# Last image's second layer: corners summed by TensorE, table writes reordered, experts' products issued ahead

## The chip, the cores and the metric

The kernel runs on one core of a Trainium2 chip. The metric is device time in microseconds (us). A core has five engines with queues of their own: TensorE (PE; its weight loads are listed apart as PEld), VectorE (DVE), ScalarE (ACT), GpSimd (POOL) and SyncE (SP), which here issues most transfers. Sixteen DMA engines move the data of all queues. TensorE reads SBUF and writes PSUM; VectorE and ScalarE read both. All data are fp32; a product of fp32 matrices shows as two matmul instructions, called passes here, and a transpose as one.

## The reference, cut to what matters

The program is two layers over 8 images of 128 channels and 32 x 32 positions (1024 tokens). The first layer (attention and a spectral mixer) takes most of the time and isn't touched. The second layer, for one image, is:

```python
# deformable convolution: 3 taps a token, 4 corners a tap, bilinear weights times a mask
h = layer_norm(x)                                  # over channels
offset, mask = conv1x3(h, off_w), sigmoid(conv1x3(h, mask_w))
for tap in range(3):
    samp = sum(corner_weight[k] * h[corner_row[k]] for k in range(4)) * mask[tap]
    out += samp @ conv_w[tap]
x = x + out + conv_b
# mixture of 8 experts, two of them kept for each token
t = layer_norm(x)
p = softmax(t @ router_w + router_b);  keep the two largest, scaled to sum 1
x = x + sum(p[e] * (t @ expert_w[e] + expert_b[e]) for e in the two)
```

## The kernel before, in words

The weights of the convolution are applied before sampling: for each tap, all tokens' `h @ conv_w[tap]` is written to a table in DRAM (`tab[tap]`, one for each tap), in four copies shifted by 0, 1, 32 and 33 rows, so that one row of 2 KB holds the four corners of a sampling point. Sampling one tap for a tile of 128 tokens is then one indirect DMA (a gather) of 128 rows of 2 KB, and a weighted sum of its four corners.

Tokens are worked on in NT = 8 tiles of 128. Second layers of images 0 to 6 run as generators between the spectral stage's instructions. The last image has no cover: when the spectral stage is over, `image` runs alone. Instructions are issued in the order of the program text; each engine takes its own in that order, and semaphores order what touches the same tile. Its steps, with the lines that matter:

- `points` turns `x2` back to tokens (`tok`), normalises, and computes `gs` (a product and a ScalarE copy, L1040, for each tile). After the fourth and the eighth tile twelve table writes each are put on a list, `write` (L1030) issues them on SP, four at a time, sorted by tap within the list as it stands. So they go out as first half tap 0, 1, 2, then second half tap 0, 1, 2. `corners` computes row numbers `idx` and weights `w`.
- `sampled` with `alone` calls `by_taps`. Its order is the first tap of all eight tiles, then taps 1 and 2 of tile 0, of tile 1 and so on: 24 points. `fetch` issues a gather (L1192, POOL) into one of three `g` tiles of three slots, some five ahead. Two points in three are added by VectorE, four `scalar_tensor_tensor` each (L1217); every third has its corners scaled by ScalarE (L1200), then a reduction (L1213) and an add (L1214).
- `norm_steps` takes statistics of the sums (L788, L789) and the inverse root on VectorE (L770 to L778), and normalises (L795). `turn_steps` transposes (L920) and copies (L923).
- `gates` makes the router's logits (L1240), the softmax and the two largest on VectorE, and turns the gates (L1275, L1277).
- Experts: for each tile two products of 512 columns into two PSUM banks `p_e` (L1137). ScalarE scales four experts of one bank (L1144), VectorE the four of the other (L1149), then reduces eight to one (L1154) and adds (L1157). After four tiles the expert biases (L1166) and the turned sums (L1169) are added up in a bank `p_out`, copied (L1173) and stored, 256 KB at a time (L1174).

The spectral stage's own accumulator is `po`, one PSUM tile of two banks (pool `op`, one buffer); its halves are copied out by ScalarE (L1585) and VectorE (L1586).

Of the kernel before, what the change touches and what calls it, by code (L numbers as in the profile page):

```python
# [11 lines left out]
F32 = mybir.dt.float32  # L12
# [6 lines left out]
P = 128  # L19
B = 8  # L20
# [782 lines left out]
class DeformAndExperts:  # L803
# [179 lines left out]
        got.extend((idx, w))  # L983
        yield

    def image(self, b, x2, x1):

        got = []
        yield from self.points(b, x2, got, True, x1)
        yield from self.sampled(b, got, True)  # L990

    def residual(self, b):

# [10 lines left out]
    def points(self, b, x2, got, alone, x1):  # L1004


        nc, sb = self.nc, self.sb
        newton = nc.vector if alone else nc.gpsimd
        tok = sb.tile([P, NT, C], F32, tag="tok", name="tok")
        yield from self.turn_back(x2, tok, x1)  # L1010
        yield
        ht = sb.tile([P, NT, C], F32, tag="ht", name="ht")
        yield from norm_steps(nc, sb, tok, ht, 1e-6, newton, not alone)
        yield 1.0 if alone else 5.0
        hc = sb.tile([C, T], F32, tag="hc", name="hc")
        yield from self.turn_steps(ht, hc)
        nc.gpsimd.tensor_tensor(tok, tok, self.cb.unsqueeze(1).to_broadcast([P, NT, C]), ALU.add)
        yield


        tab = self.tabs[b % 2]
        N = TAPS * C + TAPS * 9
        gs = sb.tile([P, NT, N], F32, tag="gs", name="gs", bufs=1)
        writes = []

        def write():
            if writes:
                i0, tap, slot, back = writes.pop(0)
                r0 = 33 - back + i0 * P
                nc.sync.dma_start(  # L1030
                    tab[tap][r0 : r0 + 4 * P, slot, :].rearrange("(i p) c -> p i c", p=P),
                    gs[:, i0 : i0 + 4, tap * C : (tap + 1) * C],
                )

        for i in range(NT):
            pg = self.bank("p_g")
            nc.tensor.matmul(
                pg[:, 0:N], hc[:, i * P : (i + 1) * P], self.gw, start=True, stop=True
            )
            nc.scalar.copy(gs[:, i, :], pg[:, 0:N])  # L1040
            if i % 4 == 3:
                writes += [
                    (i - 3, tap, slot, back)
                    for tap in range(TAPS) for slot, back in enumerate((0, 1, 32, 33))
                ]
                if alone:
                    writes.sort(key=lambda w: w[1])
            for _ in range(4 if alone else 2):
                write()
            yield 1.0 if alone else 1.5  # L1050
        while writes:
            for _ in range(4 if alone else 2):
                write()
            yield 1.0 if alone else 1.7
        po = self.bank("p_om")
        for tap in range(TAPS):
            at = TAPS * C + 9 * tap
            nc.tensor.matmul(
                po[:, 0 : 9 * NT], self.shift[tap], gs[:, :, at : at + 9],
                start=(tap == 0), stop=(tap == TAPS - 1),  # L1060
            )
        om = sb.tile([P, NT, 9], F32, tag="om", name="om")
        nc.vector.tensor_tensor(
            om, po[:, 0 : 9 * NT].rearrange("p (i k) -> p i k", k=9), self.base, ALU.add
        )
        yield
        yield from self.corners(om, got)
        got.append(tok)

    def sampled(self, b, got, alone):  # L1070

        nc, sb = self.nc, self.sb
        newton = nc.vector if alone else nc.gpsimd
        idx, w, tok = got
        x3 = sb.tile([P, NT, C], F32, tag="x3", name="x3")
        rows = [tab.rearrange("r s c -> r (s c)") for tab in self.tabs[b % 2]]
        if alone:
            yield from self.by_taps(idx, w, tok, x3, rows)  # L1080
        points = [] if alone else [(i, tap) for i in range(NT) for tap in range(TAPS)]
        fetched, here, tiles = [], [], []

        def fetch():
# [10 lines left out]
                )  # L1095
                fetched.append((i, tap))

        if not alone:
            yield 8.0
            for _ in range(4):  # L1100
                fetch()
                yield 2.6
            yield 5.0
        for i, tap in points:
            fetch()
            g = tiles[i]
# [13 lines left out]
                nc.vector.tensor_add(x3[:, i, :], x3[:, i, :], tok[:, i, :])  # L1120
            yield 2.6
        tt = sb.tile([P, NT, C], F32, tag="ht", name="tt")
        yield from norm_steps(nc, sb, x3, tt, 1e-5, newton, not alone)
        yield 1.0 if alone else 5.0
        tc = sb.tile([C, T], F32, tag="hc", name="tc")
        yield from self.turn_steps(tt, tc)
        yield
        got = []
        yield from self.gates(tc, got, 0.0 if alone else 3.0)
        gate, gt = got  # L1130
        ot = sb.tile([C, T], F32, tag="ht", name="ot")
        for i in range(NT):
            g = sb.tile([P, TAPS, 4, C], F32, tag="g", name="ge", bufs=3)
            part = g.rearrange("p t k c -> p (t k) c")[:, 0:NE]
            for grp in range(2):
                pe = self.bank("p_e")
                nc.tensor.matmul(  # L1137
                    pe, tc[:, i * P : (i + 1) * P],
                    self.ew[:, grp * 4 : grp * 4 + 4, :].rearrange("d e c -> d (e c)"),
                    start=True, stop=True,  # L1140
                )
                if grp == 0:
                    for k in range(4):
                        nc.scalar.activation(  # L1144
                            part[:, k], pe[:, k * C : (k + 1) * C], AF.Identity,
                            scale=gate[:, i, k : k + 1],
                        )
                else:
                    nc.vector.tensor_tensor(  # L1149
                        part[:, 4:8], pe.rearrange("p (k c) -> p k c", c=C),  # L1150
                        gate[:, i, 4:8].unsqueeze(2).to_broadcast([P, 4, C]), ALU.mult,
                    )
                    both = sb.tile([P, C], F32, tag="both", name="both")
                    nc.vector.tensor_reduce(  # L1154
                        both, part.rearrange("p e c -> p c e"), AX.X, ALU.add
                    )
                    nc.vector.tensor_add(x3[:, i, :], x3[:, i, :], both)  # L1157
                yield 1.3 if alone else 2.2
            if i % 4 == 3:
                if not alone:  # L1160
                    yield 3.0
                half = i // 4
                po = self.bank("p_out")
                for k in range(4):
# [9 lines left out]
                nc.sync.dma_start(self.out[b].rearrange("c h w -> c (h w)")[:, cols], ot[:, cols])  # L1174
                yield

    def by_taps(self, idx, w, tok, x3, rows):


        nc, sb = self.nc, self.sb  # L1180
        order = [(i, 0) for i in range(NT)] + [(i, tap) for i in range(NT) for tap in (1, 2)]
        got = []

        def fetch():
            n = len(got)
            if n == len(order):
                return
            if n % TAPS == 0:
                fetch.tile = sb.tile([P, TAPS, 4, C], F32, tag="g", name="g", bufs=3)
            i, tap = order[n]  # L1190
            got.append(fetch.tile[:, n % TAPS])
            nc.gpsimd.indirect_dma_start(  # L1192
                out=got[n].rearrange("p k c -> p (k c)"), out_offset=None, in_=rows[tap],
                in_offset=bass.IndirectOffsetOnAxis(ap=idx[:, i, tap : tap + 1], axis=0),
            )

        def scale(n):
            i, tap = order[n]
            for k in range(4):
                nc.scalar.activation(  # L1200
                    got[n][:, k, :], got[n][:, k, :], AF.Identity, scale=w[:, i, tap, k : k + 1]
                )

        for _ in range(5):
            fetch()
        for n, (i, tap) in enumerate(order):
            fetch()
            if n % TAPS == 0 and n + 2 < len(order):
                scale(n + 2)
            so_far = (x3 if tap else tok)[:, i, :]  # L1210
            if n % TAPS == 2:
                both = sb.tile([P, C], F32, tag="both", name="both")
                nc.vector.tensor_reduce(both, got[n].rearrange("p k c -> p c k"), AX.X, ALU.add)  # L1213
                nc.vector.tensor_add(x3[:, i, :], so_far, both)  # L1214
            else:
                for k in range(4):
                    nc.vector.scalar_tensor_tensor(  # L1217
                        x3[:, i, :], got[n][:, k, :], w[:, i, tap, k : k + 1],
                        x3[:, i, :] if k else so_far, ALU.mult, ALU.add,
                    )  # L1220
            yield 1.3

    def turn_back(self, src, dst, more):

# [132 lines left out]
class Spectral:  # L1357
# [217 lines left out]
    def mix(self, img, term, spans, mf, us, last):  # L1575
        for lo, hi, k in spans:
# [2 lines left out]
                us[:, term, :, lo:hi], last and term == 1,  # L1579
            )  # L1580

    def finish(self, img):
        x2 = img["x2"] = self.sb.tile([C, T], F32, tag="x2", name="x2")
        xv = x2.rearrange("c (h t two) -> c h two t", two=2, h=2)
# [4 lines left out]
def spectral_and_second_layer(tc, spec, layer, weights):  # L1589
# [16 lines left out]
    def second_layer(b, x1):  # L1606
        got = []
        yield from layer.points(b, imgs[b]["x2"], got, False, x1)
        rows[1].append(layer.sampled(b, got, False))

    def advance(time):
        for r, row in enumerate(rows):
# [72 lines left out]
            mf[n + 2] = spec.read_matrices(work[n + 2][1])  # L1685

    last = imgs[B - 1]
    runs = [layer.image(B - 1, last["x2"], last["tokens"]), chain(*rows[0], *rows[1])]
    while runs:
        runs = [r for r in runs if next(r, r) is not r]  # L1690

# [96 lines left out]
```

## Time and profile before

| | |
|---|---|
| three runs | 2662.8, 2663.11, 2657.89 us; median 2662.8 |
| profiled execution | 2658.17 us, span 2656.4 us, mean granted TensorE clock 0.978 |
| busy | PE 94%, DVE 70%, POOL 55%, ACT 40% |
| spectral stage ends (last `po` product) | 2525.8 us |
| first to last table write issued | 2543.08 to 2564.6 us |
| first to last gather issued | 2560.85 to 2593.2 us |
| corner sums complete | 2602.88 us |
| gates complete | 2620.2 us |
| last copy of the output ends | 2653.19 us |

Times are counted from the start of the span. In a line of the chain the columns are start, length and what ran; in a table of stretches they are the stretch, busy time and count for each engine, the granted TensorE clock as a share of full speed, the DMA engines' busy share and the rate. `<-` names what ended a wait. "SPq" is SP's queue. The ends of matmuls are modelled.

### The profile page before, as it was taken

The numbers are of one execution on the slowest core, as the hardware profiler recorded it, in microseconds if no ns is written. First come the engines' busy times: TensorE is split into PE (matmuls) and PEld (weight loads), VectorE is DVE, ScalarE is ACT, GpSimd is POOL, SyncE is SP. The second block draws the span as 40 slices with busy tenths as digits, with TensorE's granted clock in tenths as the row PEclk, the third lists the DMA queues.
The fourth block names the chain that finished last, engine by engine and source line by source line (L and its number), as shares of the span: only waits on it lengthen the run. The fifth ranks groups of instructions, "written<-read, shape, count | busy, mean of one in ns | idle before, by whom it ended". The sixth has DMA issues, their size and how long they took to land. (4 is left out here: it accounts for less than half of the span.)

```text
span 2656.4 us, 47332 instructions
## 1 busy us (share of the span) xinstructions
PE 2500.7 (94%) x18768; PEld 1750.2 (66%) x18768; DVE 1852.6 (70%) x2800; ACT 1064.2 (40%) x1982; POOL 1449.2 (55%) x1535
## 2 busy tenths in 40 slices
PE   6999999999999789999999999999999999999924
PEld 3555555555555468878778778778778778778612
DVE  3788888888888545549749748658658658658656
ACT  4676766667766311124214214224224224224222
POOL 4777777877778555446246237237337337236230
PEclk9999999999999999999999999999999999999966
DMA  1000000000000154465365266266356357256160
GB/s 30 2 18 2 18 17 2 18 2 18 10 18 18 57 165 157 145 191 176 99 189 180 91 182 192 87 183 188 98 168 201 100 154 215 92 144 213 48 182 20
DMA packets 214531, 271.29 MB, mean 102 GB/s; under 512 B 20948, under 2 KB 147092, under 8 KB 214304
## 3 DMA queue, kind: packets, MB, share of 16 engines
q1 hardware_dynamic: 197504, 212.61, 26.6%
q0 software_dynamic: 16800, 55.59, 6.3%
q8 instruction: 150, 2.46, 0.4%
q14 instruction: 77, 0.63, 0.1%
HBM read 200.22 MB, written 67.92 MB: 101 GB/s over the span
## 5 line engine op out<-in xcount | busy, mean ns | idle before, releaser
L623 POOL TENSOR_TENSOR t<-e 128x1024 f32<-128x1024 f32 x256 | 608.2, 2376 | 198.9 <-ACT e L614 198.7
L651 DVE TENSOR_TENSOR e<-e,rb 128x2048 f32<-128x2048 f32 x256 | 570.8, 2277 | 84.5 <-PE rb L644 84.5
L614 ACT ACTIVATE e<-s 128x2048 f32<-128x2048 f32 x256 | 481.1, 1879 | 253.0 <-PE s L609 250.5
L1557 POOL TENSOR_TENSOR part<-us,part 128x256 f32<-128x256 f32 x256 | 191.0, 746 | 705.6 <-ACT part L1556 698.7
L1509 PE MATMUL po<-us,mf 128*128 128x128 f32 (+2 forms) x2048 | 528.1, 381 | 5.8 <-DVE mf L1441 5.8
L1555 ACT COPY us<-p_x 128x256 f32<-128x256 f32 x256 | 95.2, 372 | 753.8 <-PE p_x L1544 740.6
L1562 DVE TENSOR_TENSOR part<-p_y,part 128x512 f32<-128x512 f32 x256 | 175.3, 685 | 289.3 <-PE p_y L1544 200.2
L1509 PEld LDWEIGHTS po<-us,mf 128*128 128x128 f32 x2048 | 308.8, 191 | 37.8 <-DVE mf L1441 6.2
L609 PE MATMUL s<-q,k 32*128 32x256 f32 x4096 | 295.9, 403 | 15.2 <-ACT e L614 14.4
L661 PE MATMUL av<-e,vt 128*32 128x256 f32 x4096 | 288.2, 389 | 4.0 <-DVE e L651 2.7
L1572 DVE TENSOR_TENSOR us<-p_z,part 128x512 f32<-128x512 f32 x256 | 174.8, 683 | 159.3 <-PE p_z L1544 159.2
L609 PEld LDWEIGHTS s<-q,k 32*128 32x128 f32 x4096 | 186.4, 185 | 137.9 <-ACT e L614 116.6
L1544 PEld LDWEIGHTS p_z<-diff,gap 128*128 128x128 f32 x1024 | 191.9, 189 | 125.3 <-issue 87.5
L1544 PE MATMUL p_z<-diff,gap 128*128 128x256 f32 x1024 | 263.4, 379 | 3.1 <-DVE base L907 3.1
L661 PEld LDWEIGHTS av<-e,vt 128*32 128x32 f32 x4096 | 101.4, 109 | 141.6 <-issue 84.7
L1091 POOL DMA_INDIRECT g<-tab,here x168 | 165.9, 988 | 43.2 <-issue 37.0
L1109 ACT ACTIVATE g<-g,w 128x128 f32<-128x128 f32 x448 | 140.1, 393 | 74.2 <-DMA g<-tab,here 73.2
L1299 POOL TENSOR_TENSOR diff<-teto 128x516 f32<-128x516 f32 x127 | 165.0, 1299 | 2.2 <-DMA teto<-in_phi_o 1.4
L1117 DVE TENSOR_REDUCE x<-g 128x128 f32<-128x1536 f32 x56 | 158.7, 2834 | 5.0
L637 DVE RECIPROCAL r<-z 128x256 f32<-128x256 f32 x64 | 112.5, 1757 | 71.3 <-PE z L630 71.1
L1544 PE MATMUL p_y<-diff,gap 128*128 128x256 f32 x512 | 152.9, 380 | 2.4 <-POOL diff L1299 2.3
L1544 PE MATMUL p_x<-teto,ht 128*128 128x256 f32 x512 | 131.4, 379 | 0.0
(268 smaller groups left out, 3708.9 us busy)
## 6 DMA issues: line engine op xcount, KB each, us to landing
mf<-mfd SPq DMA_DIRECT2D x112, 512.0 KB
tab<-gs SPq DMA_DIRECT2D x192, 256.0 KB
teto<-in_phi_o SPq DMA_DIRECT2D x127, 256.5 KB
teto<-in_phi_e SPq DMA_DIRECT2D x127, 256.0 KB
mfd<-mf SPq DMA_DIRECT2D x16, 512.0 KB
xc<-in_x SPq DMA_DIRECT2D x8, 512.0 KB
x1d<-xt SPq DMA_DIRECT2D x8, 512.0 KB
m_room<-in_M_plus SPq DMA_DIRECT2D x16, 256.0 KB
```

What stands on the lines that cost most here:

```text
L609: nc.tensor.matmul(s[:, j, c, :], img["k"][rows, hg, 2 * r + c, :], q[rows, qc * QU : (qc + 1) * QU], start=True, stop=True,)
L614: nc.scalar.activation(e.rearrange("p j c q -> p (j c q)"), s.rearrange("p j c q -> p (j c q)"), AF.Exp, scale=float(HD) ** -0.5,)
L623: nc.gpsimd.tensor_add(t, e[:, :, 0, :], e[:, :, 1, :])
L651: nc.vector.tensor_tensor(e, e, un["rb"].unsqueeze(2).to_broadcast([P, NH, 2, QU]), ALU.mult)
L661: nc.tensor.matmul(qrt["av"][32 * j : 32 * j + 32, 0:QU], img["v"][:, 2 * r + c, P * hg + 32 * j : P * hg + 32 * j + 32], un["e", r][:, j, ...
L1091: nc.gpsimd.indirect_dma_start(out=tiles[-1][:, tap].rearrange("p k c -> p (k c)"), out_offset=None, in_=rows[tap], in_offset=bass.Indirec ...
L1299: lambda: nc.gpsimd.tensor_sub(blocks[:, :, 0:2], pair, one),
L1509: self.nc.tensor.matmul(out, lhsT, rhs, start=bank not in img["opened"], stop=last, skip_group_check=True)
L1544: nc.tensor.matmul(out, weights, moving, start=start, stop=stop, skip_group_check=True)
L1557: nc.gpsimd.tensor_add(part[:, 0], mine[:, :, 0:P], part[:, 1])
L1562: nc.vector.tensor_tensor(part[:, 2:4], y[:, 0].unsqueeze(1).to_broadcast([C, 2, 2, P]), part[:, 0:2], ALU.add)
L1572: nc.vector.tensor_tensor(result(2, 4), z, part[:, 2:4], ALU.add)
```

## The change

Only the last image's second layer changes; the other seven keep their path (`sampled` loses its `alone` branches, `by_taps` goes).

- **Writes.** In `points`, alone, a write is issued before the last tile only if it is of the first tap. The order becomes first tap of both halves, then second tap of both, then third.
- **Rooms.** Gathers go into 24 rooms cut from the spectral stage's tiles (`us`, `mf`, `teto`), six ahead, none used twice.
- **Order of points.** Eight first taps, then (0,1), (1,1), (2,1), (0,2), (3,1), (1,2) and so on: the twelfth point is the first of the third tap.
- **Sums.** `sums` is a PSUM tile of two banks from the spectral pool. `tok` is put in by a product with the identity; each point's corners are scaled in place (ScalarE every third point, VectorE the others, the last shared) and added by four products with the identity. Statistics of a tile are taken from `sums` two finished tiles later, between the points; ScalarE copies each half to `x3`.
- **Experts.** Products run two tiles ahead, those of the first two tiles before the gates. Of a tile's eight, VectorE takes the first together with `x3`, ScalarE the other seven; VectorE folds 8 to 4 to 2 to 1 with adds. Biases are put into `turned` (the same two banks) during the first two tiles; each tile is turned one tile later; every two tiles are copied and stored (128 KB).

```diff
-            for _ in range(4 if alone else 2):
-                write()
+            for _ in range(4 if alone else 2):
+                if not alone or i == NT - 1 or (writes and writes[0][1] == 0):
+                    write()
...
+    def sampled_alone(self, b, got, rooms, op):
+        nc, sb, ident = self.nc, self.sb, self.ident
+        idx, w, tok = got
+        rows = [tab.rearrange("r s c -> r (s c)") for tab in self.tabs[b % 2]]
+        order = [(i, 0) for i in range(NT)] + [(0, 1), (1, 1)]
+        order += [p for i in range(2, NT) for p in ((i, 1), (i - 2, 2))] + [(NT - 2, 2), (NT - 1, 2)]
+        sums = op.tile([P, 2, 2, HT // 2], F32, tag="o", name="sums")
+        half_sums = sums.rearrange("p h a c -> p h (a c)")
+        acc = sums.rearrange("p h a c -> p (h a c)").rearrange("p (i c) -> p i c", c=C)
+        for half in range(2):
+            nc.tensor.matmul(
+                half_sums[:, half], ident,
+                tok[:, half * 4 : half * 4 + 4, :].rearrange("p i c -> p (i c)"),
+                start=True, stop=False, skip_group_check=True,
+            )
...
+        def stats(i):
+            nc.vector.bn_stats(st[:, i, :], acc[:, i, :])
+            nc.vector.bn_aggr(mv[:, i, :], st[:, i, :])
...
+        for _ in range(6):
+            fetch()
+        done = []
+        for n, (i, tap) in enumerate(order):
+            fetch()
+            g = fetched[n]
+            split = 2 if n == len(order) - 1 else 0 if n % 3 == 1 else 4
+            if split:
+                nc.vector.tensor_tensor(
+                    g[:, 0:split], g[:, 0:split],
+                    w[:, i, tap, 0:split].unsqueeze(2).to_broadcast([P, split, C]), ALU.mult,
+                )
+            for k in range(split, 4):
+                nc.scalar.activation(g[:, k, :], g[:, k, :], AF.Identity, scale=w[:, i, tap, k : k + 1])
+            for k in range(4):
+                nc.tensor.matmul(
+                    acc[:, i, :], ident, g[:, k, :], start=False,
+                    stop=(tap == TAPS - 1 and k == 3), skip_group_check=True,
+                )
+            if len(done) > 1:
+                stats(done.pop(0))
+            if tap == TAPS - 1:
+                done.append(i)
+                if i % 4 == 3:
+                    half = slice(i - 3, i + 1)
+                    nc.scalar.copy(x3[:, half, :], acc[:, half, :])
+            yield 1.3
+        for i in done:
+            stats(i)
+        rs = inverse_std(nc, sb, mv[:, :, 1], 1e-5, nc.vector)
...
+        def expert_products():
+            i = len(experts)
+            if i < NT:
+                experts.append([self.bank("p_e") for _ in range(2)])
+                for grp, pe in enumerate(experts[i]):
+                    nc.tensor.matmul(
+                        pe, tc[:, i * P : (i + 1) * P],
+                        self.ew[:, grp * 4 : grp * 4 + 4, :].rearrange("d e c -> d (e c)"),
+                        start=True, stop=True,
+                    )
+        got = []
+        for n, step in enumerate(self.gates(tc, got, 0.0)):
+            if n == 0:
+                expert_products()
+                expert_products()
+            yield step
...
+        def turn(i):
+            nc.tensor.matmul(
+                turned[:, i * P : (i + 1) * P], x3[:, i, :], ident,
+                start=False, stop=True, skip_group_check=True,
+            )
+            if i % 2:
+                cols = slice((i - 1) * P, (i + 1) * P)
+                nc.scalar.copy(ot[:, cols], turned[:, cols])
+                nc.sync.dma_start(out[:, cols], ot[:, cols])
+
+        for i in range(NT):
+            g = sb.tile([P, TAPS, 4, C], F32, tag="g", name="ge", bufs=3)
+            part = g.rearrange("p t k c -> p (t k) c")[:, 0:NE]
+            for k in range(NE):
+                pe = experts[i][k // 4][:, k % 4 * C : k % 4 * C + C]
+                if k:
+                    nc.scalar.activation(
+                        part[:, k], pe, AF.Identity, scale=gate[:, i, k : k + 1]
+                    )
+                else:
+                    nc.vector.scalar_tensor_tensor(
+                        part[:, 0], pe, gate[:, i, 0:1], x3[:, i, :], ALU.mult, ALU.add
+                    )
+            nc.vector.tensor_add(part[:, 0:4], part[:, 0:4], part[:, 4:8])
+            nc.vector.tensor_add(part[:, 0:2], part[:, 0:2], part[:, 2:4])
+            nc.vector.tensor_add(x3[:, i, :], part[:, 0], part[:, 1])
+            expert_products()
+            if i < 2:
+                for k in range(4 * i, 4 * i + 4):
+                    nc.tensor.matmul(
+                        turned[:, k * P : (k + 1) * P], self.ebm[:, k, :], gt,
+                        start=(k % 4 == 0), stop=False, skip_group_check=True,
+                    )
+            if i:
+                turn(i - 1)
+            yield
+        turn(NT - 1)
...
+    def rooms(self):
+        for _ in range(3):
+            us = self.sb.tile([C, 2, 2, HT], F32, tag="us", name="us_room", bufs=3)
+            for n in range(4):
+                yield us[:, n // 2, n % 2].rearrange("p (k c) -> p k c", c=C)
...
```

## The prediction

> **What bounds the kernel now.** I read the 40 slices of the page first: PE is at 9 tenths until slice 38, then 2 and 4. The change touches only the stretch after the spectral stage, from 2526 us, where the last image is alone. So the second view is busy time by stretch (columns: PE, PEld, DVE, ACT, POOL busy, granted clock, DMA share, GB/s):
>
> ```profile
> 2544.00:2550.00 6.00, 2.16 (x10) 1.12 (x8) 2.76 (x15) 1.66 (x4) 0.00 (x0) 1.00 0.98 282
> 2551.00:2564.00 13.00, 0.00 (x0) 0.00 (x0) 0.52 (x5) 0.00 (x0) 2.54 (x3) 0.50 0.97 276
> 2564.00:2570.00 6.00, 0.00 (x0) 0.00 (x0) 2.82 (x8) 1.27 (x4) 4.48 (x6) 0.50 1.04 337
> 2572.00:2586.00 14.00, 0.00 (x0) 0.00 (x0) 13.08 (x35) 5.05 (x16) 10.57 (x12) 0.50 0.73 205
> 2596.00:2603.00 7.00, 0.00 (x0) 0.00 (x0) 6.58 (x17) 1.15 (x4) 0.00 (x0) 0.50 0.00 1
> 2620.00:2653.00 33.00, 23.49 (x65) 12.12 (x65) 22.67 (x25) 10.40 (x35) 0.00 (x0) 0.81 0.02 8
> ```
>
> The DMA engines are full from 2544 to 2570 (table writes, then writes and gathers together); then VectorE is full until 2603; in the experts nobody is. Third, the chain that ended last:
>
> ```profile
> 2555.90 0.88 SPq L1030
> 2556.82 3.75 DMA tab<-gs
> 2560.58 0.27 issue
> 2560.85 1.05 POOL g L1192
> ...
> 2601.55 1.02 DVE both L1213
> 2602.59 0.29 DVE x L1214
> ...
> 2620.79 3.43 PE p_e L1137 x4
> 2624.24 0.70 DVE ge L1149
> 2625.04 1.92 DVE both L1154
> ...
> 2636.88 5.60 PE p_e L1137 x10
> ...
> 2652.60 0.59 ACT ot L1173
> ```
>
> The first gather waits for the sixteenth write; VectorE's sums end at 2602.88; gates are ready at 2620.2; the experts run at VectorE's 2.9 us a tile plus two starts on TensorE. Fourth, one line's waits, which decides most below:
>
> ```profile
> L1586 DVE COPY x<-po x8: 682/692/693, 1113.3 to 2526.5; 128x512 f32<-128x512 f32 x8
>   ACT x L1585: 6.8, 6
> ```
>
> L1585 and L1586 read different halves of `po` and write different halves of `x2`, yet VectorE's copy starts 0.03 us after ScalarE's ends (2526.43, 2526.46). So engines on one PSUM tile are put in program order, two readers too, and whatever part they read.
>
> **Part 1: writes reordered.** The 24 writes stay, and so does their traffic. Writes 5 to 8 now wait for the last `gs` copy (2545.81 instead of an issue at 2545.55); the 0.3 us is hidden, because DMA is still busy with write 4 until 2548.3. The first tap is complete with write 8, landed at 2552.9 in the DMA records, instead of write 16 at 2559.65. Released 1.2 us later as now, the first gather starts at 2554.1, 6.75 us earlier. POOL then issues one per 1.28 us (20 in 25.73 us).
>
> This is not kept. The twelfth gather is now the first of the third tap, and needs all 24 writes. Gather data start 3.25 us after issue (2560.85, 2564.1), so DMA is shared from 2557.3, when 14 writes are done (the fourteenth at 2557.45). Ten writes and eleven gathers of 262 KB remain, 5.5 MB; at the 337 GB/s of the mixed stretch that is 16.3 us, to 2573.6. Add 1.5 us from last data to POOL's start (2559.3, 2560.85): the twelfth starts at 2575.1 instead of its turn at 2568. Twelve more steps of 1.28 us: the last starts at 2590.5 and lands 3.4 us later, at 2593.9, against 2595.8 now. Bounds: 2568, if writes kept 283 GB/s beside the gathers; 2578, if the mixture made only 283.
>
> The rooms cost POOL nothing: they hold spectral tiles last read by 2526. They remove its wait of 2.22 us for `both`.
>
> **Part 2: sums on TensorE.** Removed: 64 L1217 at 0.373 us, eight reductions of 1.01, eight adds of 0.29, and the sixteen statistics behind them (2602.80 to 2606.06). Added per point: a scaling, 0.68 us on VectorE (L1113, 128x512) or 1.28 on ScalarE (L1200), and four products of two passes. Sixteen such passes (L1166, L1169) took 1.78 us at full clock, so a point is 0.87 us, at clock 0.50 1.72. Each alone is below or near POOL's 1.28.
>
> But `sums` is one PSUM tile, and the statistics, written between the points, read it. By L1586, statistics wait for the point just issued and the next point waits for them; VectorE's next scaling is queued behind. From point 15 every second point has this. One pair then takes 0.87 + 0.2 tail + 0.47 statistics + 0.61 scaling + 0.87 + 0.1 = 3.1 us, where POOL delivers one in 2.56. From landing at 2578.5: first scaling to 2579.2; points 12 to 15, half of them at the low clock after the gap, 6 us, to 2585.2; four pairs, 12.4, with the copy of the first half (+0.9) and one ScalarE scaling (-0.7), to 2597.8; last point 0.5 + 0.4 + 0.9, statistics 0.5, copy 0.65, two statistics and wake-ups 1.35, to 2602.1. The inverse root starts there instead of at 2606.10: **4.0 us gained**. Bounds: all at full clock, 2601.0; at 0.50 throughout, 2611.4 (the two points of a pair cost 1.7 more). `tok` as a product (four passes, at most 3.4 us) lies before 2551, while gathers are awaited.
>
> [...]
>
> **Part 3: unchanged chain.** From inverse root to gates 14.1 us (2606.1, 2620.2). TensorE has idled some 6 us, so the router's products keep 0.215 us a pass.
>
> **Part 4: experts.** Ahead of the gates run eight 512-column passes, 0.854 us each at the low clock and 0.43 after; started at 2615.1 they end near 2621.0, so the gate transpose is 0.7 us late and ScalarE starts 1.45 us after the gates (2622.59 was 2.4). Bounds of that: 0.9 and 2.5. Then each tile: `scalar_tensor_tensor` (k=0) and ScalarE's k=1..3 read one bank. In program order ScalarE waits for VectorE's k=0, which is queued behind the fold of the tile before, which waits for ScalarE's k=7. So nothing overlaps: seven activations 1.90 (L1144 steps 0.255, last 0.37), adds 0.68 (128x512), 0.42 (128x256, L1565), 0.20 step (L1157), k=0 0.354 (L1217), hops 0.18: 3.74 a tile, against 2.9. It ends 1.45 + 7 x 3.74 + 1.90 + 1.5 last fold + 0.66 turn + 0.4 copy = 32.1 after the gates; now 33.0 (2653.19): **0.9 gained**, since the late start (4.0) and the refill in the middle (3.9) go. TensorE needs 2.4 us a tile at full clock, hidden; 3.9 at 0.50, not hidden, up to 2 lost. The copies of `turned` are hidden in ScalarE's wait.
>
> **Part 5: store.** Half the bytes last: 0.3 of the 3.2 us after 2653.21, bounds 0 and 0.6.
>
> **Sum**: 4.0 + 0.9 + 0.3 = 5.2 us. Against the profiled execution (2658.17, span 2656.4) 2653.0. Two of the three runs took 2662.8 and 2663.1, one 2657.89; against the median it is 2657.6. I say 2656.
>
> **Rivals.** *Slower: the clock stays at 0.50.* These stretches of 3.41 us show when it moves:
>
> ```profile
> 2618.87:2622.28 3.41, 1.94 (x3) 0.95 (x4) 1.16 (x6) 0.27 (x1) 0.00 (x0) 0.50 0.00 0
> 2622.28:2625.69 3.41, 3.41 (x5) 1.35 (x4) 1.34 (x2) 1.14 (x4) 0.00 (x0) 0.50 0.00 0
> 2629.11:2632.52 3.41, 2.17 (x13) 1.46 (x11) 3.27 (x4) 1.14 (x4) 0.00 (x0) 1.00 0.00 0
> 2632.52:2635.93 3.41, 0.71 (x4) 0.52 (x4) 3.24 (x5) 0.00 (x0) 0.00 (x0) 1.00 0.00 0
> ```
>
> PE busy 1.94 did not raise it, 3.41 did (the next stretch has 1.00); 2.17 kept it, 0.71 lost it. The pairs fill about 2.3 of 3.41 at full clock (kept), 2.7 at half (between the rows, open). If it isn't raised in points 12 to 15, the inverse root starts at 2611.4, 5.3 late, and experts lose their 0.9 and another 1: 6 us slower, 2664 to 2669. It decides when the raise comes after about point 18. Against it: those four points fill 6.9 us without a gap. [...]
>
> *Order doesn't bind.* Columns or readers of one tile go side by side. Then points keep POOL's pace, and after the last landing come its scaling, products, tail and statistics (2593.9 + 0.4 + 0.9 + 0.2 + 0.5 + 0.3: 2596.2, 9.9 gained). A tile of experts takes ScalarE's seven steps of 0.255 and half a copy, 2.0 us: 1.5 less than 3.74 counting a share of waits for TensorE, some 10 gained over eight tiles. Together 20 us, 2638 to 2643. For it: halves of `ge` in SBUF show no such wait. Against: L1586.
>
> *Writes get through.* The share falls to the writes; the twelfth gather at 2571: 2 to 4 more, 2651 to 2654.
>
> **Numbers.** Main case 0.60, its own range 2650 to 2661; it straddles the bound of 0.2% (5.3 us), about what a measurement can tell from no change: 0.29 faster, 0.29 same, 0.02 slower. Clock rival 0.15 (0.11 slower, 0.04 same), no order 0.12 (faster), writes 0.13 (0.11 faster, 0.02 same). Together 0.52, 0.35, 0.13. The range 2648 to 2665 leaves out the no-order case and the clock's worst.
>
> **What would show it.** First gather near 2554, a wait of POOL for `tab` of some 7 us before the twelfth; VectorE's statistics waiting for TensorE; inverse root near 2602; ScalarE waiting for VectorE once a tile, tiles 3.7 us apart; clock 1.00 from about 2585. Tiles nearer 2.2, or no second wait of POOL, would make it wrong on the fast side, clock 0.50 after 2590 on the slow one.

## The result, and the profile after

The changed kernel takes 2656.8 us (median of 20 runs, 2652.3 to 2661.6), the kernel before 2659.8 us beside it (20 runs, 2656.4 to 2663.3). The ratio is 0.9988, with a 95% interval of 0.9981 to 0.9994: 3.0 us gained, between 1.6 and 5.1. That lies within the 0.2% that was called no change. The profiled execution has a span of 2653.6 us (2655.4 us in all), against 2656.4 before.

Busy time by stretch of the kernel after (columns as before: PE, PEld, DVE, ACT, POOL, granted clock, DMA share, GB/s):

```profile
2546.00:2552.00 6.00, 4.86 (x17) 2.27 (x15) 1.96 (x11) 2.23 (x5) 0.00 (x0) 1.00 0.82 238
2556.00:2569.00 13.00, 7.43 (x39) 7.14 (x40) 2.08 (x3) 2.56 (x8) 9.92 (x11) 0.56 1.05 329
2570.00:2577.00 7.00, 6.43 (x47) 5.68 (x47) 2.35 (x4) 2.56 (x8) 0.00 (x0) 1.00 0.84 288
2577.00:2596.00 19.00, 11.72 (x81) 10.80 (x80) 5.86 (x13) 5.06 (x16) 13.00 (x14) 0.91 0.65 181
```

In the third line POOL does nothing for 7 us: that is the new wait, for the 24th write. VectorE, full before, is busy for under half of every stretch. The chain that ended last, in order of time (start, length, what ran):

```profile
2569.31 6.99 DMA tab<-gs
...
2589.90 0.31 DVE st L1196
...
2597.76 2.07 PE sums L1227 x16
...
2603.82 0.18 DVE rs_v L770
...
2612.76 6.56 PE p_e L1259 x8
...
2622.76 0.29 DVE x L1302
2623.05 0.27 DVE ge L1297
2623.35 1.92 ACT ge L1293 x7
...
2650.32 0.37 ACT ot L1284
```

VectorE's statistics (L1196) stand between TensorE's products (L1227), each waiting for the other (the statistics 11.0 us in all for the products, 6 times). In the experts every piece follows the one before: ScalarE's seven (L1293), the folds (L1300 to L1302), VectorE's k=0 of the next tile (L1297), ScalarE again. What ended ScalarE's idle time before L1293 (us, times):

```profile
  DVE ge L1297: 12.2, 7
```

The last image's own time is best counted from its first table write, since the spectral stage ahead of it ends between 2523 and 2533 us from one execution to the next, although the change doesn't touch it (in the traces of before and after TensorE's instructions up to there come in the same order). In us after the first write, one profiled execution each (`e6` is the changed kernel once more; the others follow below):

| kernel | last gather starts | inverse root | gates to end | end |
|---|---|---|---|---|
| before | 49.2 | 63.0 | 36.2 | 113.4 |
| after | 46.7 | 57.8 | 35.7 | 107.6 |
| e6, the same kernel | 48.2 | 63.2 | 34.7 | 112.0 |
| e1 | 47.7 | 64.0 | 24.3 | 102.5 |
| e2 | 47.9 | 55.7 | 35.1 | 104.9 |
| e3 | 42.5 | 63.3 | 34.7 | 112.1 |
| e4 | 47.5 | 79.5 | 35.2 | 128.8 |
| e5 | 48.4 | 76.3 | 35.1 | 125.5 |
| e7 | 47.5 | 55.2 | 25.1 | 94.4 |
| e8 | 47.5 | 55.5 | 24.9 | 94.5 |
| e9 | 47.2 | 72.3 | 35.4 | 121.8 |
| e10 | 43.1 | 53.9 | 24.3 | 92.3 |
| e11 | 41.2 | 58.7 | 24.9 | 97.7 |
| e12 | 47.9 | 55.7 | 24.4 | 94.6 |

So the profiled pair shows 113.4 - 107.6 = 5.8 us gained in this part, about the forecast. The two executions as wholes differ by only 2.8 us (2658.17 and 2655.40), because the changed kernel's first write came 2.9 us later (2546.01 against 2543.08), within the spread of the spectral stage; the medians of twenty, in which that spread should even out, show 3.0. The experiments ask two things: where the other 2 to 3 us went, and whether the two chains above are there for the reason given, program order on one PSUM tile.

### The profile page after: what moved, and what is told of

Read it like the earlier page. It is cut to its first block, busy times and chain, and to the rows that moved or that the text cites. A ratio compares the mean times of both kernels' runs of the same rounds, so it can differ in the third digit from the quotient of the medians.

```text
span 2653.6 us, 47720 instructions
## 1 busy us (share of the span) xinstructions
PE 2538.2 (96%) x18964; PEld 1779.5 (67%) x18964; DVE 1828.6 (69%) x2744; ACT 1071.9 (40%) x2012; POOL 1447.0 (55%) x1535
```

## The experiments

Each was compared with runs of the kernel before on the same chip; ratios are to that kernel, with 95% intervals. The changed kernel's own is 0.9988.

### e1: VectorE's k=0 of the next tile ahead of the folds

```diff
+        parts = [first(0)]                 # first(i): scalar_tensor_tensor of k=0
         for i in range(NT):
+            for k in range(1, NE): nc.scalar.activation(parts[i][:, k], ...)
+            if i + 1 < NT: parts.append(first(i + 1))
             nc.vector.tensor_add(part[:, 0:4], part[:, 0:4], part[:, 4:8])
```

> VectorE's k=0 of tile i+1 is put ahead of the three folds of tile i in VectorE's queue; nothing is added or taken away, and every PSUM tile still has the same two readers. Theory (program order on one PSUM tile): in the changed kernel ScalarE starts a tile 0.3 us after VectorE's k=0, which stands behind the last fold (2622.76, 2622.97, 2623.35), so that ScalarE's 1.92 us and VectorE's folds never overlap and a tile takes 3.78 us. With k=0 ahead they overlap: a tile takes ScalarE's 1.92 and a share of its copies of the output, about 2.2 us, seven tiles gain 11 us, the whole 2646 us against 2656.8 (ratio to the kernel before 0.9945 to 0.996). Rival 1 (a bank admits one reader at a time, whatever the order): nothing changes, 3.78 a tile, 2656.8. Rival 2 (TensorE's products bind, since at half clock a tile's four passes and its turn take 3.9 us, and at full clock nearly 2.0): a tile no shorter than 3.3 us, at most 3.5 us gained.

Measured 0.9945 (0.9928 to 0.9962), against 0.9988: some 11 us. Experts on ScalarE and VectorE in the timeline of e1 (start, length, engine, line, operation; in brackets the idle time before and what ended it):

```profile
2619.24 5.71 ACT L1300 ACTIVATE ge<-p_e,gates 128x128 f32<-128x128 f32 x21
2621.20 0.69 DVE L1305 TENSOR_TENSOR ge<-ge 128x512 f32<-128x512 f32 x1 [1.88 <-ACT ge L1300]
2622.59 0.34 DVE L1290 SCALAR_TENSOR_TENSOR ge<-p_e,gates,x 128x128 f32<-128x128 f32 x1
```

ScalarE runs 21 activations, three tiles, without a pause, while VectorE folds beside it. Tile starts go from 2619.24 to 2635.30 for the eight, 2.29 us apart; from the gates to the end it takes 24.3 us instead of 35.7. The same instructions touch the same banks; only their order in VectorE's queue is new. The rivals as they were put, nothing changed and no tile under 3.3 us, are out.

### e2: statistics of the copy in SBUF

```diff
-            nc.vector.bn_stats(st[:, i, :], acc[:, i, :])
+            nc.vector.bn_stats(st[:, i, :], x3[:, i, :])   # four tiles after each copy
```

> The statistics of the third layer norm read the copy of the sums in SBUF that the kernel makes anyway, four tiles at a time, instead of the sums in PSUM; so between the points nothing but two copies reads the PSUM tile. Theory (points and statistics of one PSUM tile take turns, 3.1 us a pair): the points follow the gathers; from the last landing (50.0 us after the first table write) come scaling 0.5, products 1.2, copy 0.7, four statistics 1.8 and wake-ups 0.2, so the inverse root starts 54.3 us after the first write instead of 57.8, 3.5 us gained, 2653.3. Rival (the points are late for VectorE's own queue or for the DMA, and the statistics only stand beside them): under 1 us gained, 2656 to 2657.

Measured 0.9970 (0.9959 to 0.9982), some 5 us under the changed kernel. In its profile the inverse root starts at 55.7, against 54.3 expected. Its end of the sums in the timeline:

```profile
2594.95 0.59 ACT L1235 COPY x<-sums 128x512 f32<-128x512 f32 x1 [0.98 <-PE sums L1227]
2595.56 0.29 DVE L1196 BATCH_NORM_STATS2 st<-x 128x6 f32<-128x128 f32 x1 [1.87 <-ACT x L1235]
```

The statistics now wait for the copy alone, as the theory has it, and in all four profiles with this edit (e2, e7, e8, e12) the inverse root starts at 55.2 to 55.7. Against the changed kernel's 57.8 that is 2.1 to 2.6 us, under the 3.5 expected. The rest of the 5 us is what the changed kernel loses in other executions (e6, next) and these four didn't; why they didn't isn't shown.

### e6: the changed kernel once more

> The changed kernel itself, once more, beside the others on one chip. Its first profiled execution had the first write at 2546.0 and the end 107.6 us after it; e1, whose sums are the same code, had the inverse root at 64.0 us after the first write instead of 57.8, with a stall of 1.7 us at 2586.3 and the clock at 0.50 for 6.8 us behind it. Theory (the sums lose their clock in some executions, by a stall of a few us): the inverse root between 58 and 66 us after the first write, executions spread over 6 us or more. Rival (e1's stall came from its own change): again near 57.8, and the spread is that of the start of the tail alone.

Measured 0.9992 (0.9982 to 1.0002). Its inverse root starts at 63.2, not 57.8: e1's 64.0 was no effect of e1's edit. In two of three executions of the same sums, then, the whole gain of this step is gone. It goes in three pieces.

The first piece lies before the statistics. The first of them starts 40.7 us after the first write in the changed kernel's first execution, 42.6 in e6 and 42.7 in e1. The twelfth gather came 0.9 and 0.8 us later, and the four points behind it took 6.5 and 6.6 us instead of 5.5, with the clock, lost in the gap before them (TensorE idle for 5.1 and 4.5 us, and for 3.7 in the first execution), low for two of its steps instead of one. A step is 3.41 us: in the traces of before and after every stretch at one clock, but for the last one recorded, is a whole multiple of 3.413 us (3.41 to 23.89 within the last image's part of the changed kernel). The first such step behind the gap, in the first execution and in e6:

```profile
2581.17:2584.59 3.42, 3.42 (x16) 3.42 (x17) 0.82 (x2) 1.28 (x4) 2.81 (x3) 0.50 0.69 184
```

```profile
2580.96:2584.38 3.42, 2.25 (x10) 2.25 (x11) 1.39 (x2) 0.06 (x1) 2.78 (x3) 0.50 0.68 184
```

Where the points filled the stretch from its start (3.42) the next one had 1.00; where they began 1.0 to 1.2 us into it (2.25; 2.38 in e1) the next one still had 0.50. In these three executions, then, it went by where the first point fell in the clock's steps.

The second piece is a stall. The half copy of e6 and a statistic of e1, in their timelines, came 1.9 and 1.7 us after the products that they need have ended by the trace's own times (2594.35 and 2586.34):

```profile
2596.29 0.59 ACT L1237 COPY x<-sums 128x512 f32<-128x512 f32 x1 [6.68 <-remote]
```

```profile
2588.01 0.30 DVE L1196 BATCH_NORM_STATS2 st<-sums 128x6 f32<-128x128 f32 x1 [3.77 <-remote]
```

"Remote" says that the profile found no releaser. The semaphore that TensorE counts up shows it. In e1 its last three steps before the statistic come at 2586.51, 2587.22 and 2587.98, 0.7 us apart, where two steps in e6 before its stall are 0.22 apart (2591.23, 2591.45); in e6 the step before the copy comes at 2596.27. So it is TensorE that was late; the matmuls' times are modelled.

The third piece is the clock again. Stretches of 3.41 us, in the steps in which it moves: the changed kernel's first execution,

```profile
2591.41:2594.83 3.42, 2.24 (x18) 1.89 (x17) 0.84 (x4) 1.76 (x5) 2.14 (x3) 1.00 0.73 202
```

and e6:

```profile
2591.20:2594.61 3.41, 1.84 (x15) 1.46 (x13) 1.67 (x4) 0.00 (x0) 2.62 (x3) 1.00 0.65 210
2594.61:2598.03 3.42, 1.10 (x8) 0.97 (x8) 0.00 (x0) 1.74 (x6) 0.77 (x2) 1.00 0.53 153
2598.03:2601.44 3.41, 2.90 (x14) 2.88 (x14) 1.06 (x3) 1.77 (x7) 0.00 (x0) 0.50 0.00 0
```

In these stretches PE busy 1.84 to 2.24 of 3.41 was followed by 1.00; 1.10, with the stall in it, was followed by 0.50, and eight passes took 2.05 us (from 2598.59) instead of 1.16 (from 2593.19). In e1 the stretch with the stall has 0.61, and the 6.8 us after it are at 0.50. Against the first execution e6 is 2.0 us late at the first statistics, 4.0 at the half copy and 5.4 at the inverse root; e1 is 2.0, 4.6 and 6.2.

### e3: gathers tap by tap

```diff
-        order = [(i, 0) for i in range(NT)] + [(0, 1), (1, 1)] + ...
+        order = [(i, tap) for tap in range(TAPS) for i in range(NT)]
```

> The gathers go tap by tap (all of tap 0, of tap 1, of tap 2) instead of mixing taps 1 and 2 from the ninth on; statistics are left as they are. Theory (the first gather of the third tap waits for the 24th write, wherever it stands; the two queues share the DMA engines evenly, so that the 24th write ends at the same time): that gather is now the 17th and not the 12th, POOL waits some 2 us at it instead of 7, the last gather starts 40.2 us after the first write instead of 46.7. The eight last points have statistics each, about 1.95 us a point, and the inverse root starts some 52 us after the first write instead of 57.8: 2651. Rival (five more gathers ahead of that wait take their bytes from the writes, 0.78 us each): the 24th write ends 3.9 us later, the last gather starts some 44 us after the first write, 2 us gained at most, which the statistics may eat: 2655 to 2658.

Measured 0.9977 (0.9966 to 0.9987). The last gather starts at 42.5, between theory (40.2) and rival (44): POOL starts the 17th 3.05 us after the 16th, instead of 1.26. But the inverse root comes at 63.3. TensorE went through two stretches, 7 and 3.6 us long, in which it took one instruction per 0.70 us with no wait that the profile shows, and the clock fell to 0.50 three times while the sums ran (eight passes took 1.13 us from 2594.9, 2.07 from 2600.2). The 0.1% by which it is ahead of the changed kernel is within the intervals. So the gathers come out half-way: the last of the writes ended 31.9 us after the first began, 1 to 2 us later than in the three executions above (29.9 to 30.9), where the rival says 3.9. What was gained there is lost on TensorE.

### e4: the writes in the order of before

```diff
-                if not alone or i == NT - 1 or (writes and writes[0][1] == 0):
-                    write()
+                write()
```

> Only the order of the table writes is put back: twelve writes of the first four tiles go out before the second four are computed, all else as in the changed kernel. Theory (the 24 writes bind the twelfth gather, and an earlier first gather only lengthens POOL's wait): the first gather starts 17.8 us after the first write instead of 9.9, the wait before the twelfth goes from 7 us to nothing, and the last gather starts 0 to 1 us later; the whole 2656.8 to 2658. Rival (the earlier first gather is what the change gains): the last gather starts 6 us or more later, 2663.

Measured 1.0039 (1.0025 to 1.0054): 13 us slower than the changed kernel, which neither side expected. The gathers did as the theory says: the first starts at 17.3 us after the first write instead of 9.9, no break before the twelfth, and the last at 47.5, as in the changed kernel. What went wrong is TensorE. Busy time by stretch, and then what TensorE waited for from 2577 to 2597.3 (us in total, times, longest):

```profile
2577.30:2597.20 19.90, 5.79 (x19) 3.88 (x17) 3.04 (x5) 3.83 (x12) 13.43 (x14) 0.60 0.67 192
2597.20:2606.00 8.80, 8.25 (x53) 8.06 (x53) 0.47 (x3) 0.00 (x0) 0.00 (x0) 0.75 0.00 0
```

```profile
PEld sums L1226 <- issue: 15.6, 12, 1.8
```

19 passes in 20 us, weight load and matmul each 0.70 us after the other, with their operands there ("issue": nothing that the profile shows). When the last gather has landed (51.5 us after the first write, 2597.2), 53 passes follow in 8.8 us. A transfer of TensorE's instructions (16 KB; between two of them the trace of before has 255 matmuls and weight loads at the median), due by its usual distance about when the writes began, is seen 28 us later, at 2576. That suggested a cause, and e5 tests it.

### e5: e4, and idle products that bring that transfer forward

```diff
+        idle = self.bank("idle")
+        for _ in range(30):     # ahead of the second layer norm's turn
+            nc.tensor.matmul(idle[:, 0:256], self.ident, self.gw[:, 0:256], start=True, stop=True)
```

> The writes in the order of before (as in e4), and 30 products of 256 columns into a bank that nobody reads, in TensorE's idle 7 us before the second layer norm's turn. In e4 TensorE took one instruction per 0.70 us from 2577.3 to 2597.2, some 117 instructions after the first product into the sums, with its operands there, and was at full pace only when the last gather had landed; its 16 KB instruction transfers come every 240 to 250 instructions, and the one due about 34 instructions before that first product (2548) was seen only at 2576, behind writes and gathers. Theory (supply of instructions: TensorE's next 16 KB stand behind the table traffic on the DMA engines): the 60 added instructions bring that transfer forward to some 2535, when the DMA engines are idle; the run of 0.70 us steps at this place is gone, the inverse root starts 58 to 66 us after the first write instead of 79.5, and the whole is 10 us or more faster than e4, 0.998 to 1.001 of the kernel before. Rival (the steps have another cause, such as the clock or a wait that the trace does not show): the steps stay, 1.003 to 1.005. Beside it: with TensorE kept busy its clock stays at 1.00 into the 16 passes of L1037, which take 3.5 us instead of 6.6, and the first write comes some 2 us earlier against the end of the spectral stage.

Measured 1.0048 (1.0031 to 1.0064). The transfer came at 2534, as meant, and the steps of 0.70 us stayed, from 2581.6 to 2599.4, again until about when the gathers had landed (the last one was issued at 2596.2). The theory of one late transfer has fallen. The fill was also mis-sized: 30 products of fp32 are 60 passes and took 13.1 us, where 7 us were to be filled, so that the first write came 21.2 us after the spectral stage's last product, instead of 17.6 in the changed kernel.

### e9: e4 with half the products

```diff
+            nc.vector.tensor_add(g[:, 0:2], g[:, 0:2], g[:, 2:4])
-            for k in range(4):
+            for k in range(2):
```

> e4 (writes in the order of before) with half the products: VectorE first adds the second two of a point's four scaled corners to the first two (128x256, 0.42 us), and TensorE adds two instead of four. e5 put the instruction transfer at 2534 and the 0.70 us steps stayed, so its theory has fallen; but they began some 30 instructions later than in e4. Theory (TensorE's instructions come too slowly while gathers follow each other without a break, and what counts is how many it needs): 24 points need 96 instructions instead of 192, less than the 117 after which the steps began in e4; they are gone or take a few us, the inverse root starts 56 to 60 us after the first write instead of 79.5, 0.998 to 1.000 of the kernel before. Rival (the steps hang on the time, from 32 us after the first write until the last gather has landed at 51.5, whatever is in the program): a point then needs 4 x 0.70 = 2.8 us where gathers come every 1.28 us, the inverse root starts 64 us or later, 1.000 to 1.002.

Measured 1.0020 (1.0009 to 1.0032). The steps begin 8 us later than in e4, but they come, from 2586.3 to 2597.8, and the inverse root is at 72.3: the rival's side. The number of instructions alone is not the cause.

### e7, e8, e10, e11: combinations

e7 is e1 and e2 together; e8 adds the fill of e5; e10 adds the order of e3 to e7; e11 adds to e10 the halved products of e9, with copies of two tiles at a time.

> k=0 of the next tile ahead of the folds (e1) and statistics of the SBUF copy (e2) together. Theory (both are waits in a row on the path that sets the end): the gains add, 0.9945 and 0.997 against the changed kernel's 0.9988: 0.9927, some 16 us under the changed kernel. Rival (the first gain is partly given back where the second one starts, as the clock falls to 0.50 between them): 0.994 to 0.9955.

> e7 and the 30 idle products of e5. Theory (supply of instructions, and the clock before the first write): first write 2 us earlier, and no execution with a run of 0.70 us steps, so 2 us at the median and up to 6 in the slow executions: 0.991 to 0.992. Rival (without the writes of before the transfer comes through in time anyway): only the 2 us of the clock, 0.992.

> e7 (k=0 ahead, statistics of the copy) with the gathers tap by tap as in e3. In e3 the last gather started 42.5 us after the first write instead of 46.7 to 48.2, but two runs of 0.70 us steps, the pairs and a clock of 0.50 put the inverse root at 63.3. Theory (without the statistics between the points the earlier gathers come through): last gather at 42.5, landing 3.3, scaling 0.5, products 1.2, copy 0.7, statistics 1.8, wake-ups 0.2, inverse root at 50 us instead of 55.2; 0.991 against 0.993 of e7. Rival (the steps come back, as in e3, some 7 us in all): inverse root at 55 or later, 0.993 to 0.995.

> e10 with half the products as in e9, and the copies two tiles at a time. Theory (fewer instructions for TensorE, so no steps, and the clock does not matter, since two products take 0.3 us at full and 0.6 at half clock): last gather at 42.5, landing 3.3, scaling 0.5, addition 0.4, products 0.6, copy 0.4, two statistics 0.9, wake-ups 0.3, inverse root at 49 us, executions within 5 us of each other, 0.990 to 0.991. Rival (VectorE, with 0.42 us more a point, becomes late for the gathers): inverse root at 53 or later, 0.992 to 0.994.

e7: 0.9930 (0.9913 to 0.9946). The gains of e1 and e2 add up, 0.9927 expected. e8: 0.9938 (0.9921 to 0.9956). From the first write on it is e7 (94.5 against 94.4 us); the fill took 13.1 us here too, and what the clock won behind it (5.8 us for the sixteen passes of `gs` instead of 6.6) was lost by that. e10: 0.9934 (0.9916 to 0.9952). Its profile has the shortest end of all, 92.3 us, although 6 us of 0.70 us steps are in it, as the rival said; its inverse root, 53.9, is between theory (50) and rival (55), and the median is that of e7. e11: 0.9921 (0.9908 to 0.9934), 2642.9 us against 2663.5 before, the fastest that was run, though its interval overlaps e7's. Neither account of e11 holds. In its profile, which is of the slowest of its six runs (2647.3):

```profile
2583.80:2592.20 8.40, 2.52 (x9) 1.61 (x7) 3.02 (x7) 0.40 (x2) 4.98 (x6) 0.66 0.68 195
2592.20:2606.50 14.30, 9.11 (x31) 7.05 (x31) 6.92 (x24) 4.42 (x14) 0.00 (x0) 0.50 0.00 0
```

The steps are back for 8.4 us, nine passes, and the points that have piled up then take 14.3 us one after the other at clock 0.50, with VectorE busy for half of it. So VectorE isn't full, as the rival had it, though TensorE waits for one of its adds before most points.

### e12: e7 with the clock kept up for the router

```diff
+        for _ in range(20):     # behind the last product into the sums
+            nc.tensor.matmul(idle[:, 0:256], ident, self.gw[:, 0:256], start=True, stop=True)
```

> e7 (k=0 ahead, statistics of the copy) and 20 products of 256 columns into a bank that nobody reads, behind the last product into the sums: TensorE is idle there for 5.8 us (2601.8 to 2607.65 in e7), its clock goes to 0.50 at 2605 and comes back only at 2618.7, with the experts. Theory (the cold clock is on the path: p_turn ends 0.3 us late, the router's sixteen passes take 3.44 us, the eight expert passes ahead end 1.2 us behind the gates): the clock stays at 1.00, the router's passes take 1.8 us, gates 12.1 us after the inverse root instead of 14.1, ScalarE's first expert 0.7 us behind them instead of 1.5; 2.8 us, 0.992 against 0.993 of e7. Rival (the products come at the low clock in most executions, since the sums have lost it before, take 8.6 us and hold up p_turn by 2 to 3 us): 0.9935 to 0.995.

Measured 0.9929 (0.9915 to 0.9942), as e7. The chain:

```profile
2601.47 8.64 PE idle L1240 x40
...
2611.22 1.95 PE p_l L1340 x16
```

Again 20 products are 40 passes, 8.6 us in a gap of 5.8. `p_turn` starts 6.1 us after the inverse root instead of 3.45, 2.6 us late, which is the rival's delay; but the clock was at 1.00, the router's passes took 1.95 us instead of 3.44, ScalarE starts 0.65 us after the gates instead of 1.5, and gates are only 0.35 us late. So the cold clock cost this part 2.3 us before the gates and 0.8 after them, and by the author's estimate a fill of half the size would win most of that. That wasn't run.

## Why the prediction was right, and where it wasn't

The time was met, 2656 forecast and 2656.8 measured, but two errors cancel in it. The gain was put at 5.2 us and is 3.0 (1.6 to 5.1). And 2656 with a gain of 5.2 stands on 2661.2 for the kernel before, between its profiled execution and the median of three runs; over twenty runs it is 2659.8. More chance was given to a gain over 0.2% than to one within, and it was within.

**Part 1, writes.** Right. First gather 9.9 us after the first write (11.0 forecast: 2554.1 less 2543.08), the twelfth at 31.2 (32.0) behind POOL's wait of 7 us, the last at 46.7 (47.4). e4 confirms that the order of the writes moves the last gather by less than 1 us, so what that end gained over 49.2 lies outside the reordering. The step's forecast effect on the gathers held; what it failed to see is that the break in the gathers, counted as mere loss, goes together with TensorE's undisturbed run (below).

**Part 2, sums.** This is the term that was mis-sized. The mechanism holds: statistics and points take turns on one PSUM tile, 3.24 us a pair (statistics at 2586.66 and 2589.90, then 2596.61 and 2599.85) against 3.1, and e2, which takes the statistics off the tile, gains. The order went by the whole tile, as was read from L1586: the statistic at 2586.66 is of the first token tile, in the first bank, and TensorE's products that it waits for, up to 2586.63, are of the fifth, in the second. So an order within each bank alone is out here. The inverse root was forecast at 2602.1, 59.0 us after the first write; measured 57.8 once, and 63.2 and 64.0 in the two other executions of this code, against 63.0 before. A gain of 4.0 was forecast; the three executions give 5.2, -0.2 and -1.0.

Two terms about the clock failed. "Half of them at the low clock" for points 12 to 15 (6 us forecast) came out in the first execution (5.5 us), while in the others the clock rose one step later (6.5 and 6.6) and the twelfth gather was later too, together 2.0 us. And "kept" in the clock rival: the pairs' fill kept the clock (2.23 of 3.41 in e6, from 2587.79), as its row of 2.17 said, but a stall of 1.7 to 1.9 us, with which TensorE was idle for 2.6 to 2.8, was followed by 0.50, and such stalls came in two of three. The fill of 2.7 at half clock that was left open came out both ways: 2.71 did not raise the clock in e1 (from 2589.14; the next stretch has 0.50), 2.73 did in e4 (from 2615.25; the sixteen passes from 2619.16 then took 2.05 us). The rival had 0.15, with another place (no raise in points 12 to 15; the raise came, if late) and a higher price (6 us slower than before; e6 ends 1.4 us sooner). In e6 idles of 1.2 and 1.3 us before the pairs (2589.83, 2593.19) left the clock at 1.00; it fell behind the one of 2.6 us.

**Part 3.** Right: 14.1 us from inverse root to gates in all but e12.

**Part 4, experts.** The order was right, and it is the larger finding: tiles 3.78 us apart against 3.74 forecast, and e1 shows that moving one instruction per tile gives some 11 us. "No order" was rightly a rival with the gain of 10 us; only, the order binds, and is avoided by program order. The net 0.9 came out as 0.2 in this execution (gates to last copy 32.8 against 33.0): the eight passes ahead took 6.56 us, all but the last 0.6 us at the low clock, ScalarE started 1.7 us after the gates instead of 1.45, and the last turn took 0.81 instead of 0.66. In e6 ScalarE started 0.64 after the gates. The bounds, 0.9 and 2.5, were a little narrow below.

**Part 5, store.** Right: 2.9 us after the last copy against 3.2.

So in the first profile the parts give 5.2 + 0.0 + 0.2 + 0.3 = 5.7 us, and in e6, the same kernel, 112.0 against 113.4, 1.4 us. The medians' 3.0 lies between. That the later twelfth gather, the clock and the stall make the difference between these executions is read from their traces; no run sets one of them by itself. How often each happens can't be said from three traces, and what causes the stall is open.

## What to carry to other kernels

Where two engines read one PSUM tile in turn, look at which instruction of the one the other waits for and what is queued in front of it: here one VectorE instruction behind three folds cost 1.5 us a tile, and issuing it three places earlier gave more than three times what the whole change gave. The price of the sums on TensorE, at a fill of 2.2 of 3.41 us, hung on the clock: eight passes took 1.16 us at 1.00 and 2.05 at 0.50 (e6), and the inverse root came at 57.8 us in the execution without a stall, at 63.2 and 64.0 in the two with one. So cost such a step at both clocks and profile more than one execution. Count fp32 fills in passes, not in products: 30 products were 60 passes and 13.1 us (e5, e8), 20 were 40 and 8.6 us (e12).

## What the runs showed of the hardware that was not expected

TensorE fell to one instruction per 0.70 us while nothing that the profile shows held it: 20 us in e4, 18 in e5, 11.5 in e9, 8.4 in e11, 6 in e10, 7 and 3.6 in e3, and three steps in e1's stall. The clock alone isn't what held it in e4: the steps begin at 2577.3, and it is at 1.00 until 2581.1. Most of these stretches end about when the last gather in flight has landed (e4: last gather issued at 2593.3, landed at 2597.2, full pace at 2597.2; e9: issued at 2593.5, full pace at 2597.8). The long ones came in the kernels whose gathers follow each other with no break over 4.1 us; with POOL's break of 8 to 9 us before the twelfth gather (the changed kernel, e1, e2, e6, e7, e8, e12) there was none over 2 us. The two go together in thirteen profiles; that isn't shown to be the cause: a single late instruction transfer (e5) and the number of instructions (e9) were tried and don't explain it, and what does stays open.
